# One kernel for a four-layer Perceiver: causal attention by tiles of 128 rows, expert routing by pairs of tiles through a table of token numbers, and cross-attention queries made one tile at a time

## The chip, the cores and the metric

The kernel runs on one core of one Trainium2 chip (trn2). The metric is the device time of one execution in microseconds (us), with the median over runs taken. The profile comes from one further execution of the same program; times inside it are counted from the start of its span.

Engines are named as the profile names them: PE is TensorE (PEld its weight loads), DVE is VectorE, ACT is ScalarE, POOL is GpSimd, SP is SyncE. Each of them runs its instructions in the order of the program that was built for it. SP, ACT and POOL can also issue DMAs.

## The reference, cut to what matters

Sixteen sequences of 64 tokens with 256 features pass through four layers, each with a cross-attention to a context of 1024 tokens of 192 features, a second sublayer and a feed-forward sublayer. All of it is fp32. The parts that the change touches are these:

```python
x = x + L0_xattn(ln(x), ctx)   # one head of 256, 1024 keys
x = x + L0_attn(ln(x))         # causal, 16 heads of 16, q and k RMS-normed over 256 and scaled by ln_w
x = x + L0_ffn(ln(x))          # 8 experts, best 2 of each token, plus a shared expert
x = x + L1_xattn(ln(x), ctx)   # 16 narrow heads of 16, 1024 keys
...
x = x + L1_ffn(ln(x))          # 8 experts, best 1 of each token
...
x = x + L2_ffn(ln(x))          # 8 experts, best 2, at most 160 tokens each
```

Both mixtures of L0 and L1 drop no token: every token goes to each of its experts, and the results come back weighed by the gates.

## The kernel before

The 1024 tokens are eight tiles of 128 rows (`NT = 8`), two sequences in each. The residual `xs` stays in SBUF. One Python object, `Net`, writes the layers one after another. A planner of the framework orders the instructions of every engine by the dependencies and its own estimates of cost. Only inside `manual_schedule(engines={PE})` is PE's order the order in which the code is written; the other engines are still ordered by the planner there.

**L0_first** holds the cross-attention and the causal attention of layer 0. The cross-attention goes by tiles: in step `n` of a loop over `NT + 2` it makes the `scores` of tile `n`, transposes the weights of tile `n - 1` (`keys_first`) and averages the context with them (`averaged`), and projects tile `n - 2` (`by_features`, `output`). Each step reads 3 MB of context, two of the four pairs of context buffers. Between these pieces stand calls of `attn.go()`, seven in a full step. Each of them runs the generator `chunk` in `causal_attention` up to its next `yield`. One chunk of 256 rows (two tiles) is in work at a time, and it starts when both its tiles have their cross-attention. It goes on to the first norm of the feed-forward (`htok`, `hT`) and to the gate logits. PSUM holds one buffer of scores, tag `sc`, which both attentions use in turn, two buffers `o`, two `t` and two `misc`. What is left of the chunks after the loop runs alone until half of them are done, and the first half of the shared expert (`swiglu`, 512 rows) then fills in.

**L0_ffn** routes all 1024 tokens at once. Softmax, the two largest experts, the rank of each token in its expert (`ranks`, a prefix sum by matmul) and the table of blocks (`blocks`: each expert gets a whole number of blocks of 128 slots, 23 blocks in all) are one chain of small DVE operations. `scatter` then writes every token's row of 1 KB to its slot in the DRAM buffer `hs`, which was filled with zeros before. That is one indirect DMA by POOL for each tile and each of the two choices, 16 in all. Each of the 23 blocks gathers its expert's weights by POOL (`wa` 11 KB and `wb` 6 KB a partition, three buffers of each), reads its 128 rows of `hs` by a plain DMA of SP (`hb`, `read_slots`), transposes them to `dT`, and does its matmuls `gu` and `po`. The block's result is written to `ys`, and at the end `take_back` gathers each token's rows from there, 16 indirect DMAs, each followed by one DVE operation that adds to `xs`.

**L1_xattn** starts with the keys and values of the first sequence (`keys_values(0)`), normalizes all eight tiles (`norm_x`), adds the bias to them, and makes the queries of all 1024 rows in two halves (`queries(half)`), with copies `qs[1]` whose partitions are swapped by a DMA. Then it loops over 64 steps of a sequence and four heads. **L1_ffn** routes as L0_ffn does with one choice: 8 scatters, then 15 blocks. **L2_ffn** scatters into fixed slots of `hs`.

Of the kernel before, what the change touches and what calls it, by code (L numbers as in the profile page):

```python
# [10 lines left out]
F32 = mybir.dt.float32  # L11
# [29 lines left out]
class Net:  # L41
# [4 lines left out]
    def __init__(self, tc, a):  # L46
        self.tc, self.nc, self.a = tc, tc.nc, a
        self.flip = 0
        self.n_pT = 2
        self.spare_dve = False  # L50
        self.halves = None

# [173 lines left out]
    def keys_first(self, p):  # L226

        pT = self.lp.tile([128, NK, 128], F32, tag="pT", bufs=self.n_pT, name="pT")
        for g in range(2):
# [4 lines left out]
            if g or self.spare_dve:  # L234
                self.nc.scalar.copy(pT[:, 4 * g : 4 * g + 4, :], ps)  # L235
            else:
                self.nc.vector.tensor_copy(pT[:, 0:4, :], ps)  # L237
        return pT
# [27 lines left out]
    def pack_L0_room(self):  # L266

        self.slot()
        return (
            self.carve(128, 2, 4, 2 * S), self.carve(128, 2, CHUNK), self.carve(128, 2, D),  # L270
            [self.carve(128, 2, D) for _ in range(2)],
            [self.carve(128, 2, 4, S) for _ in range(4)],
            [self.carve(128, 4, 128) for _ in range(4)],
        )

    def L0_first(self):

# [5 lines left out]
        self.spare_dve = True  # L283
        self.more_ctx(self.lp)
# [6 lines left out]
        with self.tc.manual_schedule(engines={mybir.EngineType.PE}):  # L291
# [23 lines left out]
            def scores(i):  # L315
                ctx = ctxs.pop(i) if i in ctxs else fetch(i)
                sc = self.lps.tile([128, KEYS], F32, tag="sc", bufs=1, name="sc")

                for kh in range(2):
                    keys = bass.ts(kh, 512)  # L320
                    for ch in range(2):
                        for par in range(2):
# [4 lines left out]
                            )  # L327
                return ctx, self.exp_rows(sc)

            def averaged(i, ctx, pT):  # L330
                o = self.misc([128, CD + 1])
                for t in range(NK):
                    for par in range(2):
# [3 lines left out]
                        )  # L337
                return self.averages(o, CD + 1)
# [16 lines left out]
            for n in range(NT + 2):  # L355
# [5 lines left out]
                if held is not None:  # L361
                    i, ctx, p = held
                    pT = self.keys_first(p)
# [3 lines left out]
                attn.go()  # L367
# [6 lines left out]
                attn.go()  # L374
                held = got
                if n == NT - 1:

                    nc.sync.dma_start(
                        self.hs.rearrange("(n p) d -> p n d", p=128),
                        self.zero.unsqueeze(1).to_broadcast([128, SLOTS // 128, D]),  # L380
                    )
            del self.ctxT[2:], self.ctx[2:]
            shared = self.swiglu(
                *self.shared, 384, self.add_to_x, 0, lambda: self.lps.tile([128, 512], F32, tag="t", bufs=2, name="gu")
            )
            while attn.go() and attn.done < NT // 2:
                pass
# [4 lines left out]
        self.spare_dve = False  # L392
# [209 lines left out]
    def causal_attention(self, wqkv, wproj):  # L602
# [4 lines left out]
        s = SimpleNamespace(ready=0, next=0, done=0, work=None)  # L607
        sb = self.sb
        room = []

        lw = sb.tile([128, 2, 2], F32, name="lw")
        for c in range(2):
            nc.vector.tensor_scalar(lw[:, c, :], self.pair4, self.col("L0a_lnw", c), None, ALU.mult)
        sel, own = self.pair_masks(sb)
        self.logits = self.act.tile([128, NT, E], F32, tag="logits", name="logits")
        after = {}

        def chunk(g):
            if not room:
                room.extend(self.pack(ahead=False))  # L620
            qs, kT, v, qks, p16, p16T = room
            qs = qs.rearrange("p c b (h q) -> p c b h q", h=2)
            os = []
            for t in range(2):
                x = self.xs[:, 2 * g + t, :]
                mv, rs = self.norm_tile(x, 1e-5)
                os.append(sb.tile([128, D], F32, tag="os", bufs=2, name="os"))
                nc.vector.tensor_scalar(os[t], x, mv[:, 0:1], rs, ALU.subtract, ALU.mult)
            yield
            hT = sb.tile([128, 2, CHUNK], F32, tag="hTs", name="hTs")  # L630
            for t in range(2):
                self.evict(hT[:, :, t * 128 : (t + 1) * 128], self.transposed(os[t]))
            yield
            for t in range(2):
                cols = slice(t * 128, (t + 1) * 128)
                ps = self.misc([128, 2, D])
                self.mm(ps.rearrange("p a b -> p (a b)"), [(hT[:, c, cols], wqkv[:, c, :512]) for c in range(2)])
# [1554 lines left out]
```

## Time and profile before

| what | value |
|---|---|
| median of 3 runs (range) | 3132.53 us (3132.1 to 3138.62) |
| profiled execution, its own time | 3130.54 us |
| its span, first to last instruction | 3128.8 us |
| mean granted TensorE clock | 0.936 |
| PE, DVE, ACT, POOL busy | 2750.3, 1463.2, 1010.6, 310.5 us |
| cross-attention of L0 on PE, first scores | from 29.87 us |
| last `xs` of the causal attention | 259.67 us |
| first matmul of the 23 blocks (`gu<-dT,wa`) | 327.56 us |
| last result of those blocks (`yb`) | 539.18 us |
| both halves of the first scores of L1_xattn there | 599.5 us |
| first matmul of the 15 blocks of L1_ffn (`ph<-dT,wa`) | 1280.98 us |

The time and the span differ by 1.7 us, which lie around the span. The stages follow each other, so each has limits of its own: the page's busy shares are averages over stages of very different kinds. A PE that is busy in a stage is not always at full speed: the granted clock stands beside it.

### The profile page before, as it was taken

The numbers are of one execution on the slowest core, as the hardware profiler recorded it, in microseconds if no ns is written. First come the engines' busy times: TensorE is split into PE (matmuls) and PEld (weight loads), VectorE is DVE, ScalarE is ACT, GpSimd is POOL, SyncE is SP. The second block draws the span as 40 slices with busy tenths as digits, with TensorE's granted clock in tenths as the row PEclk, the third lists the DMA queues.
The fourth block names the chain that finished last, engine by engine and source line by source line (L and its number), as shares of the span: only waits on it lengthen the run. The fifth ranks groups of instructions, "written<-read, shape, count | busy, mean of one in ns | idle before, by whom it ended". The sixth has DMA issues, their size and how long they took to land.

```text
span 3128.8 us, 42567 instructions
## 1 busy us (share of the span) xinstructions
PE 2750.3 (88%) x16976; PEld 1987.6 (64%) x16976; DVE 1463.2 (47%) x2986; ACT 1010.6 (32%) x2160; POOL 310.5 (10%) x425
## 2 busy tenths in 40 slices
PE   6887899699999879788999999496999888887899
PEld 3654787366666536675777776494777566665668
DVE  2553111566666672124444443322345656658591
ACT  1221121255555411122322332021225445455330
POOL 1112221200000010320011000202000000000000
PEclk9897899799999988799999999698999999998999
DMA  9612774201010100761211111373113212122110
GB/s 231 187 41 73 276 275 179 60 31 32 21 32 23 47 1 27 271 217 35 60 42 41 52 51 51 126 248 112 51 41 87 70 41 88 47 72 58 52 37 7
DMA packets 149408, 273.18 MB, mean 87 GB/s; under 512 B 16511, under 2 KB 103258, under 8 KB 142426
## 3 DMA queue, kind: packets, MB, share of 16 engines
q1 hardware_dynamic: 127418, 170.90, 18.6%
q0 software_dynamic: 14784, 93.26, 8.3%
q10 hardware_dynamic: 7008, 6.29, 0.6%
q8 instruction: 134, 2.20, 0.3%
q14 instruction: 64, 0.52, 0.1%
HBM read 247.83 MB, written 20.45 MB: 86 GB/s over the span
## 4 chain that ended last, share of the span: by engine, by line
PE 65%; DVE 10%; issue 7%; ACT 4%; DMA 3%; POOL 2%; SPq 1%; ACTq 0%; DVEq 0%; POOLq 0%
PE misc L65 10%; PE sc L498 8%; PE halves L65 7%; PE gu L65 6%; PE po L65 4%; PE misc L233 4%; PE ps_h L65 4%; PE ps_t L233 3%; PE sc L65 2%; PE misc L844 2%; PE o L892 2%; PE misc L858 2%; DVE x L1832 2%; ACT p L223 2%; PE misc L177 2%
## 5 line engine op out<-in xcount | busy, mean ns | idle before, releaser
L221 DVE TENSOR_REDUCE nmx<-sc 128x1 f32<-128x1024 f32 x264 | 311.7, 1219 | 243.9 <-PE sc L498 148.1
L223 ACT ACTIVATE p<-sc,nmx 128x1024 f32<-128x1024 f32 x264 | 294.0, 1115 | 323.7 <-DVE nmx L221 322.4
L498 PE MATMUL sc<-ctxT,qp 128*128 128x512 f32 (+1 forms) x1024 | 353.9, 600 | 0.0
L498 PEld LDWEIGHTS sc<-ctxT,qp 128*128 128x128 f32 (+1 forms) x1024 | 138.2, 189 | 153.4 <-issue 151.9
L158 POOL TENSOR_TENSOR ln_rs<-ln_ve,nhalf 128x1 f32<-128x1 f32 x120 | 66.7, 561 | 1531.3 <-DVE ln_ve L156 1267.0
L65 PE MATMUL halves<-ctx,pT 128*128 128x193 f32 x1024 | 189.3, 339 | 9.2 <-DVE xs L85 4.1
L65 PEld LDWEIGHTS halves<-ctx,pT 128*128 128x128 f32 x1024 | 177.2, 200 | 12.0 <-DVE xs L85 4.6
L65 PE MATMUL misc<-ctx,pT 128*128 128x193 f32 x1024 | 179.3, 327 | 0.9 <-DVE qT L463 0.9
L65 PEld LDWEIGHTS misc<-ctx,pT 128*128 128x128 f32 x1024 | 167.7, 191 | 2.8 <-DVE qT L463 1.6
L233 PE MATMUL ps_t<-ident,p 128*128 128x128 f32 x1088 | 148.0, 279 | 18.1 <-ACT p L223 10.5
L1832 DVE TENSOR_TENSOR_SCAN x<-da,x 128x512 f32<-128x512 f32 x128 | 152.2, 1213 | 2.1 <-ACT da L1822 1.4
L235 ACT COPY pT<-ps_t 128x512 f32<-128x512 f32 x182 | 103.8, 582 | 149.0 <-PE ps_t L233 148.6
L1822 ACT ACTIVATE da<-rep,al 128x252 f32<-128x252 f32 x256 | 114.8, 498 | 111.1 <-DVE x L1832 90.2
L233 PEld LDWEIGHTS ps_t<-ident,p 128*128 128x128 f32 x1088 | 128.2, 144 | 32.1 <-ACT p L223 13.4
L233 PE MATMUL misc<-ident,p 128*128 128x128 f32 x1024 | 136.8, 279 | 7.1 <-ACT p L223 6.7
L65 PE MATMUL gu<-dT,wa 128*128 128x128 f32 (+1 forms) x1104 | 133.5, 280 | 4.0 <-issue 3.5
L65 PEld LDWEIGHTS gu<-dT,wa 128*128 128x128 f32 (+1 forms) x1104 | 125.7, 185 | 12.7 <-ACT yb L1207 6.3
L233 PEld LDWEIGHTS misc<-ident,p 128*128 128x128 f32 x1024 | 110.1, 141 | 32.7 <-ACT p L223 13.6
L65 PE MATMUL po<-wb,hid 128*128 128x256 f32 x516 | 124.5, 388 | 0.0
L65 PE MATMUL ps_h<-r,w 128*128 128x256 f32 x512 | 115.3, 385 | 0.0
L65 PEld LDWEIGHTS ps_h<-r,w 128*128 128x128 f32 x512 | 97.8, 192 | 16.6 <-issue 2.9
L237 DVE COPY pT<-misc 128x512 f32<-128x512 f32 x128 | 88.2, 689 | 42.5 <-PE misc L233 36.7
(446 smaller groups left out, 4374.7 us busy)
## 6 DMA issues: line engine op xcount, KB each, us to landing
ctx<-in_ctx SPq DMA_DIRECT2D x48, 768.0 KB
ctxT<-in_ctxT SPq DMA_DIRECT2D x48, 512.0 KB
w<-in_L2f_W SPq DMA_DIRECT2D x24, 1024.0 KB
rep<-dus SPq DMA_DIRECT2D x256, 64.0 KB
ctxT<-in_ctxT SPq DMA_DIRECT2D x16, 768.0 KB
ctxT<-in_ctxT SPq DMA_DIRECT2D x96, 128.0 KB
hb<-hs SPq DMA_DIRECT2D x46, 128.0 KB
ys<-yb ACTq DMA_DIRECT2D x46, 128.0 KB
```

The lines of the kernel that those rows point to most:

```text
L65: self.nc.tensor.matmul(out, lhsT, rhs, start=n == 0, stop=n == len(pairs) - 1)
L158: nc.gpsimd.tensor_tensor(rs, ve, self.nhalf, ALU.pow)
L177: self.nc.tensor.transpose(ps[:, c, :], o[:, c * 128 : (c + 1) * 128], self.ident)
L221: self.nc.vector.tensor_reduce(nmx, sc, AX.X, ALU.max, negate=True)
L223: self.nc.scalar.activation(p, sc, AF.Exp, bias=nmx, accum_out=sums)
L233: self.nc.tensor.transpose(ps[:, u, :], p[:, at : at + 128], self.ident)
L235: self.nc.scalar.copy(pT[:, 4 * g : 4 * g + 4, :], ps)
L237: self.nc.vector.tensor_copy(pT[:, 0:4, :], ps)
L498: nc.tensor.matmul(sc[u][:, bass.ts(kh, 512)], qp[n][par][rows, h : h + 2, :].rearrange("p h q -> p (h q)"), ctx[0][rows, at], start=n == ...
L844: nc.tensor.matmul(ps[kh], wk[:, kh, cols], cT[:, bass.ts(kh, 512)], start=True, stop=False)
L1822: nc.scalar.activation(da[:, g, :, 1:], now[j][:, 0, :].rearrange("p (b s) -> p b s", s=S)[:, :, 1:], AF.Exp, scale=al[:, col : col + 1],)
L1832: nc.vector.tensor_tensor_scan(flat, da.rearrange("p g b s -> p (g b s)"), flat, 0.0, ALU.mult, ALU.add)
```

## The change

The causal attention goes by tiles of 128 rows, and up to two tiles are in work at once. The generator `tile` has about twenty pieces, some of them empty, and nine calls of `go()` stand in a full step of the cross-attention, some of them in the middle of its scores and averages. `sc` gets two buffers, the separate `o` goes (its results use `sc` too), and some DVE operations are merged or moved to ACT. The squared norm weight now stands in the queries, and the keys are a plain copy.

After each second tile a generator `routing` is queued behind the tiles. It writes the two tiles' normalized rows to `hs` in the order of the tokens by plain DMAs, makes their logits, softmax, best two and ranks (with a running count `seen`), and scatters the *token numbers*, 4 bytes each, to a DRAM table in which every expert has a region of 1024 places (`place` + `region`).

`blocks` reads one row of 128 token numbers per block from that table by an indirect DMA of POOL that waits for all scatters (`who`), transposes it and keeps it as `tokens`. Each block then gathers its rows of `hs` by POOL with these numbers, in place of SP's plain read. L1_ffn is built the same way, with all its tiles at once. The fixed slots of L2_ffn move to a buffer of their own, `caps`, and only these are filled with zeros.

The shared expert runs in four parts of 256 rows: two in the drain of L0_first, two in L0_ffn. L1_xattn makes the queries of tiles 0 and 1 ahead of its loop and those of tile `i + 2` in the loop, while tile `i` is at work; its bias comes ahead of the first keys.

The core of the diff:

```diff
     def keys_first(self, p, between=lambda: None):
...
+            if not g:
+                between()
...
-                sc = self.lps.tile([128, KEYS], F32, tag="sc", bufs=1, name="sc")
+                sc = self.lps.tile([128, KEYS], F32, tag="sc", bufs=2, name="sc")
...
+                    if not kh:
+                        attn.go()
...
-                    nc.sync.dma_start(
-                        self.hs.rearrange("(n p) d -> p n d", p=128),
-                        self.zero.unsqueeze(1).to_broadcast([128, SLOTS // 128, D]),
-                    )
+                    for n in range(E * CAP // 128):
+                        self.zeros(self.caps[n * 128 : n * 128 + 128])
...
-            while attn.go() and attn.done < NT // 2:
-                pass
+            shared = chain(*(self.shared_part(k) for k in range(2)))
             while attn.go():
                 next(shared, None)
...
+        def tile(i):
...
+            nc.vector.tensor_tensor(qk, ps, rr.unsqueeze(2).to_broadcast([128, 2, D]), ALU.mult)
...
+            nc.scalar.copy(kT, pt[:, 1])
+            yield
+            yield
+            sc = [self.lps.tile([128, 2, 512], F32, tag="sc", bufs=2, name="sc") for _ in range(2)]
...
+            for _ in range(3):
+                yield
...
+            o = self.lps.tile([128, 2, 512], F32, tag="sc", bufs=2, name="o")
...
+            self.add_to_x(i, po)
+            if i % 2:
+                s.behind.append(routing(i // 2))
+            yield
...
+        def routing(g):
...
+            for t in range(2):
+                i = 2 * g + t
+                nc.sync.dma_start(self.hs[i * 128 : (i + 1) * 128], normalized(i, self.htok[:, i, :]))
...
+            for _ in self.route(self.routed, ps, 2 * g):
+                yield
+                yield
 
         def go():
-            if s.work is None and s.next < NC and s.ready >= 2 * s.next + 2:
-                s.work = chunk(s.next)
+            if len(s.work) < 2 and s.next < s.ready:
+                s.work.append(tile(s.next))
                 s.next += 1
-            if s.work is not None and next(s.work, s) is s:
-                s.work = None
-            return s.work is not None or s.next < NC
+            for w in list(s.work):
+                if next(w, s) is s:
+                    s.work.remove(w)
+            if s.behind and next(s.behind[0], s) is s:
+                s.behind.pop(0)
+            return s.work or s.next < NT or s.behind
...
-        def queries(half):
+        def queries(i):
+            mv, rs = self.norm_tile(self.xs[:, i, :], 1e-5)
...
+            nc.gpsimd.tensor_tensor(self.xs[:, i, :], self.xs[:, i, :], bias, ALU.add)
+            yield
...
+            for m in range(2):
+                self.mm(ps[:, m, :], [(wq[:, c, m * 128 : (m + 1) * 128], hT[:, c, :]) for c in range(2)])
...
             for r in range(2):
+                nc.sync.dma_start(qs[i][1][64 * r : 64 * r + 64], qs[i][0][64 - 64 * r : 128 - 64 * r])
...
+            biases()
             for piece in keys_values(0):
                 piece()
-            biases()
-            self.norm_x()
-            for i in range(NT):
-                nc.gpsimd.tensor_tensor(self.xs[:, i, :], self.xs[:, i, :], bias, ALU.add)
-            for half in range(2):
-                queries(half)
+            for i in range(2):
+                for _ in queries(i):
+                    pass
...
+    def route(self, r, logits, first, weighed=None):
...
+        p = self.gate_softmax(logits)
...
+        place = r.place[:, tiles, :]
+        rank = self.ranks(both, r.seen, place)
+        yield
+        rank()
+        for k, m in enumerate(masks):
+            t = self.gate("s_t", n)
+            nc.vector.tensor_tensor(t, place, self.region.unsqueeze(1).to_broadcast([128, n, E]), ALU.add)
+            nc.vector.tensor_tensor(t, t, m, ALU.mult)
+            slot, _ = self.over_experts(t, ALU.add, "s_r")
+            nc.vector.tensor_copy(r.at[k][:, tiles], slot)
+        yield
+        for k in range(len(masks)):
+            self.scatter(r.table, r.at[k], tiles, r.group, lambda i: self.token[:, i : i + 1])
...
-    def blocks(self, count, n_blocks):
+    def blocks(self, seen, table, n_blocks):
+        ps = self.misc([128, E])
+        self.mm(ps, [(self.ones, seen)])
...
+        who = self.lp.tile([n_blocks, 128], F32, name="who")
+        self.behind_scatters(
+            self.gather_rows(who, table.rearrange("(n p) o -> n (p o)", p=128), row[:n_blocks])
+        )
+        ps = self.misc([128, n_blocks])
+        nc.tensor.transpose(ps, who, self.ident[:n_blocks, :n_blocks])
+        tokens = self.lp.tile([128, n_blocks], I32, name="tokens")
+        nc.vector.tensor_copy(tokens, ps)
...
     def block_tokens(self, j):
         hb = self.lp.tile([128, D], F32, tag="hb", bufs=3, name="hb")
-        self.read_slots(hb, slice(j * 128, (j + 1) * 128))
+        self.gather_rows(hb, self.hs, self.tokens[:, j : j + 1])
...
     def L1_ffn(self):
...
+        for i in range(NT):
+            nc.sync.dma_start(self.hs[i * 128 : (i + 1) * 128], self.htok[:, i, :])
...
-        self.scatter(at, "L1f")
```

## The prediction

> **What bounds the kernel now.** I read the page's busy shares, split the span by stages with the windows view, then read each engine's timeline where PE has gaps. Windows (us, then busy us and instructions of PE, PEld, DVE, ACT, POOL; granted clock, DMA share, GB/s):
>
> ```profile
> 30.00:66.00 36.00, 26.31 (x134) 11.36 (x135) 6.05 (x11) 6.01 (x9) 0.55 (x1) 0.86 0.93 235
> 66.00:260.00 194.00, 162.72 (x1170) 110.70 (x1164) 96.10 (x249) 47.37 (x110) 29.21 (x37) 0.84 0.40 115
> 260.00:328.00 68.00, 39.08 (x121) 22.93 (x122) 17.59 (x74) 8.63 (x13) 22.66 (x24) 0.77 0.32 115
> 328.00:539.00 211.00, 206.98 (x1421) 178.03 (x1420) 37.09 (x103) 42.29 (x125) 37.45 (x40) 0.99 0.69 251
> 539.00:600.00 61.00, 29.65 (x96) 13.60 (x96) 28.53 (x74) 6.05 (x11) 26.88 (x37) 0.75 0.31 81
> 600.00:1070.00 470.00, 464.57 (x4388) 290.05 (x4386) 303.70 (x399) 259.57 (x468) 3.83 (x7) 1.00 0.09 27
> ```
>
> The blocks of L0 and the loop of L1_xattn are PE's (98% and 99%, full clock). Context loads bound the first 36 us. The rest, 66 to 328 and 539 to 600, belongs to waits: there PE is 84%, 57% and 49% busy, at a clock of 0.84 to 0.75. PE's timeline names them:
>
> ```profile
> 163.30 1.99 PE L65 MATMUL misc<-rT,sel 8*128 8x256 f32 x8
> 237.71 3.68 PE L65 MATMUL sc<-w 32*128 32x64 f32 x32 [1.48 <-DVE sm L680]
> 251.22 3.78 PE L65 MATMUL misc<-rT,sel 8*128 8x256 f32 x8
> 323.84 0.66 PE L177 MATMUL misc<-ident,hb 128*128 128x128 f32 x2 [23.57 <-DMA hb<-hs]
> 572.20 3.78 PE L844 MATMUL misc<-ctxT,w 128*128 128x512 f32 x4 [26.64 <-DVE kT L849]
> 597.48 2.07 PE L65 MATMUL sc<-kT,qs 32*128 32x512 f32 x4 [4.31 <-DMA qs<-qs]
> ```
>
> The same eight matmuls take 1.99 us in mid-loop and 3.78 us in the drain: gaps also cost clock. The long wait for `hb` is POOL's queue:
>
> ```profile
> 295.88 1.20 POOL L1189 DMA_INDIRECT wa<-in_L0f_w,rows  x1 [33.49 <-issue]
> 297.39 1.01 POOL L1173 DMA_INDIRECT hs<-htok,s_at  x1 [0.30 <-DVE xs L85]
> ...
> 316.57 0.97 POOL L1173 DMA_INDIRECT hs<-htok,s_at  x1 [0.31 <-DMA hs<-htok,s_at]
> 317.85 0.99 POOL L1189 DMA_INDIRECT wb<-in_L0f_w2r,rows  x1 [0.30 <-issue]
> ```
>
> Sixteen scatters at 1.28 us hold it for 20 us. A 1 KB and an 11 KB row cost POOL the same 0.95 to 1.2 us, so 4 bytes should too.
>
> **Part 1: L0_first.** I count PE's work from 66.0 us at full clock, from timeline pieces. Cross-attention: five scores at 3.66, six transposes at 1.07, six averages at 2.85, seven outputs with features at 1.6: 53 us. A chunk of 256 rows: qkv 5.7, three transposes 3.9, scores 4.0, averages 2.2, shares 2.6, projection 2.0, routing's transposes and logits 2.2: 22.6, four times 90. Half the shared expert (24 `gu` at 0.43, 24 `po` at 0.23): 16. Together 159. Before, all this ended at 283, so 217 us: 58 are lost. Two tiles in work, staggered by half a tile, and empty pieces put 2 to 3 calls of other PE work behind each hand-over to DVE or ACT. Counting the calls: nine in a full step, 63 from the first ready tile to the end of the loop; a tile takes 20, so tiles 0 to 4 and most of 5 lie in the loop. That leaves 118 us of work to it; at 87% PE (above the 84% of now, since single waits remain) it ends at 66 + 136 = 202. The drain has 39 us of PE work, but tile 7 is alone at the end, where its chain (about 26 us from norm to sum by its rows) is bare: 44 us. The last sum is at 246, not 260. Bounds: 232 (PE at 97%) and 262 (no overlap gained; both attentions still take turns in `sc`).
>
> The small routing operations of three pairs (about 40 at 0.2 us, 8 us of DVE each) move under this: DVE is at 96 of 194 us, so I cost them at nothing; uncovered they cost 24. `hs` goes out on SP, eight plain DMAs; SP's next loads are two steps ahead.
>
> **Part 2: from the last sum to the first block.** Before: 259.67 to 327.56, 68 us. After, a chain: two norms, transposes, logits 5.4 (259.67 to 265.13 now); softmax to both masks, 4.9 on 64 columns now, 4.3 on 16; running counts, rank matmul, `place`, places 3.0: 12.7. Four scatters 5.1, landing 1.5 (last one ended 317.54, SP issued `hb` at 319.0): 19.3. Then `who` 1.0 + 1.9 (the gather `back`, end of issue 543.06 to use 544.91), transpose and copy 1.0, `hb` 2.8, transpose and eviction 1.1: 27 with empty queues. PE has two parts of the shared expert (16 us) under it.
>
> The queues aren't empty: `rows` is ready at about 13, so weights of 2.25 MB a block (6.1 us at 370 GB/s, what 320 to 332 us moved) are issued while POOL waits for the scatters. Here a row and a rule part. Row: `hb` on SP, issued at 319.3 with five weight gathers outstanding, reached PE 4.5 us later. The Trainium skill, "DMA: Bandwidth & Descriptors", section "Queues, rings and completion order": the engines take turns between queue rows, but within a row's ring descriptors go in order. SP's read shared with the weights; POOL's `who` and `hb` would stand behind them. By the row, block 0 starts at 27 + 2 = 29; by the rule at 43, if three blocks' weights are ahead (18.2 us). No run here shows a small gather behind large ones. The planner issued what was ready, earliest in the code first; so I put `wa`, `wb` of block 0 ahead of `who` and those of block 1 ahead of `hb`: 35. First block at 246 + 35 = 281 instead of 327.6: **46 less**, 31 to 62 likely. The two new waits stand in POOL's order: `who` for the scatters, `hb` for `tokens`, up to 1.5 and 4 us. Behind them are the weights of blocks 1 and 2, needed 9 and 18 us later, so this delay is covered by block 0.
>
> **Part 3: the blocks.** POOL gets 23 and 15 gathers at 1.25 us more (37 of 211 us busy now), SP loses as many. The next `hb` buffer is free when an old block is transposed, before its weights' buffer, so it should be issued first. Costed at nothing; its cover is the three-deep `hb`.
>
> **Part 4: L1_xattn.** Before, the loop runs from 597.5, since `kT` waited in DVE's order behind nearly all additions of `take_back`, then 9.6 us of PE for all norms' transposes and queries. After, with two tiles' norms only, POOL's 16 gathers take 20.5 us (542.1 to 562.6), `kT` follows at about 564, the rest of keys and values 9.6, two tiles' queries with their swap DMA 5: 578, 19 earlier. But six tiles' queries (8 matmul records at 0.12 and transposes, 1.5 us) enter a loop where PE is full: 9 back. Net 11. From 8 to 28, if `kT` is ordered early.
>
> **Part 5: L1_ffn.** Places no longer wait for `first` (3 us sooner), still 8 scatters, then `who`, `tokens`, and `hb` behind two blocks' weights: first matmul at 1279 to 1283, now 1280.98. Zero, from 4 gained to 8 lost. L2_ffn's chain stays; zeroing 1.3 instead of 3.4 MB has DMA slack beside it.
>
> **Sum.** 46 + 11 + 0 = 57. The profiled execution is 3130.5 with 1.7 us around its span: 3073.5 there; the median is 2.0 higher: 3075.
>
> **Rivals.**
> *Less overlap* (0.22): drain and waits stay, last sum at 262, tail 35, L1_xattn 8: 31 + 8 less a few for L1_ffn, about 3096. For it: one shared `sc` pair, DVE's fixed order. Against: the waits named above are single hand-overs, which another tile fills.
> *More* (0.18): last sum at 236, no weights ahead, `kT` early: 328 - 265 = 63, 28, 3: about 3040. For it: little PE work is needed in the tail. Against: POOL issued weights early before.
> *Slower* (0.05): in the blocks `hb` stands in POOL's ring behind weights that wait for a buffer, so a block starts only when later weights have landed. Over 38 blocks the gain of 57 is gone at 1.5 us each, that is a pace of 10.7 for 9.2 us in L0; 2 us each give 3151. For it: SP's queue had no such neighbour. Against: three buffers and DMA at 0.69.
> *Nothing in sum* (0.01): POOL's and DVE's order put the last pair's routing behind the shared expert and `take_back`, as now, so that parts 1 and 4 come back as waits: 3132.
>
> **Numbers.** The forecast case has 0.54; its range is 3060 to 3090. With the others, 3040 to 3108 leaves about 2 in 10 out. 0.2% (6 us) is about what a measurement can tell: faster 0.94, same 0.01, slower 0.05.
>
> **What would show it.** Last `xs` of tile 7 near 246 with no `sc` wait over 2 us; POOL with four, not 16, scatters before `wa`; `hb` at about 33 us after that sum; block pace 9.2; the L1_xattn loop from about 532 (597.5 less 46 and 19), and longer by 9. Wrong if PE in 66 to 200 stays at 84%, if `who` lands after all three weights, if blocks wait for `hb`, or if `kT` still ends the start of L1_xattn.

## The result, and the profile after

The change made the kernel a little faster: 3119.81 us in the median of 20 runs, against 3132.30 us for 20 runs of the kernel before. The ratio is 0.9967, with a 95% interval from 0.9957 to 0.9977. The forecast was 3075 us with a range from 3040 to 3108: the sign was right, and 57 us were forecast where about 12 came. The profiled execution has a span of 3123.7 us (3128.8 before) and lies some 6 us above the median of its kernel, as one sample may. One of the 20 runs of the changed kernel lasted 5600.49 us; it counts as slow and stands outside the ratio.

The same views as before, now of the changed kernel. First the stages (us, then busy us and instructions of PE, PEld, DVE, ACT, POOL; granted clock, DMA share, GB/s), cut where the stages end now:

```profile
66.00:264.00 198.00, 164.80 (x1296) 110.60 (x1291) 104.33 (x326) 59.45 (x139) 41.50 (x50) 0.85 0.43 101
264.00:303.00 39.00, 21.83 (x91) 17.49 (x89) 14.11 (x76) 4.43 (x10) 13.29 (x14) 0.78 0.59 136
303.00:514.00 211.00, 206.70 (x1424) 177.10 (x1424) 37.36 (x104) 42.84 (x126) 57.70 (x62) 1.00 0.71 260
514.00:566.00 52.00, 21.83 (x80) 11.20 (x82) 21.91 (x66) 4.47 (x7) 23.95 (x33) 0.69 0.22 64
566.00:1052.00 486.00, 478.94 (x4492) 300.65 (x4490) 317.13 (x433) 262.45 (x474) 6.74 (x11) 0.99 0.10 29
```

The blocks (third row) are as long as before with 20 us more of POOL. L1_xattn's loop (last row, cut wide) is 10 us longer: from the end of its first scores to its last `o<-pT,v` it takes 487.1 us, before 477.0. The tail of L0_first (second row) went from 68 to 39 us. But the first row, which was to end at 246, is still at a clock of 0.85 and PE 83% busy, and the start of L1_xattn (fourth row) has PE at 42%. PE's timeline names what it waited for:

```profile
208.74 2.11 PE L698 MATMUL pt<-ident,w 128*128 128x128 f32 x8 [7.70 <-ACT w L691]
257.37 2.12 PE L698 MATMUL pt<-ident,w 128*128 128x128 f32 x8 [4.21 <-ACT w L691]
295.16 0.29 PE L1246 MATMUL misc<-ident,who 23*128 23x23 f32 x1 [11.60 <-DMA who<-table,row_p]
295.38 7.09 PE L67 MATMUL misc<-w,hid 128*128 128x256 f32 x24
302.31 0.38 PE L179 MATMUL misc<-ident,hb 128*128 128x128 f32 x2
303.37 5.72 PE L67 MATMUL gu<-dT,wa 128*128 128x128 f32 x48 [0.68 <-issue]
541.35 2.07 PE L67 MATMUL misc<-w,bv 128*128 128x256 f32 x4 [27.87 <-DVE bv L815]
565.62 2.08 PE L67 MATMUL sc<-kT,qs 32*128 32x512 f32 x4 [0.26 <-DMA qs<-qs]
1253.86 0.25 PE L1246 MATMUL misc<-ident,who 15*128 15x15 f32 x1 [27.77 <-DMA who<-table,row_p]
```

Two of these waits are for `who`, the new gather from the table. POOL's timeline shows that it was not late by its own issue: between `wa` and `who` POOL stands still for 9.28 us (10.46 us in L1_ffn, the last line, where the profile names the scatters as what it waited for).

```profile
278.89 0.95 POOL L1269 DMA_INDIRECT table<-token,route_at  x1 [0.30 <-issue]
280.15 1.00 POOL L1291 DMA_INDIRECT wa<-in_L0f_w,rows  x1 [0.30 <-issue]
290.43 1.20 POOL L1291 DMA_INDIRECT who<-table,row_p  x1 [9.28 <-issue]
291.92 0.97 POOL L1291 DMA_INDIRECT wb<-in_L0f_w2r,rows  x1 [0.30 <-issue]
295.94 0.94 POOL L1291 DMA_INDIRECT hb<-hs,tokens  x1 [3.04 <-DVE tokens L1248]
1249.10 0.91 POOL L1291 DMA_INDIRECT who<-table,row_p  x1 [10.46 <-DMA table<-token,route_at]
```

The last scatter's issue ends at 279.84, and `who` starts at 290.43: 10.6 us for the landing (until the written bytes are in memory and a reader may start), where the prediction had 1.5. In L1_ffn it is 11.7 us.

Every kernel below is compared by these stages, each taken from one profile of its own, in us: the last `xs` of L0_first; from there to the first matmul of L0's blocks (the tail); from the last `yb` of the blocks (its start on ACT) to the first `sc<-kT,qs` of L1_xattn; and in L1_ffn from the first operation on the gate logits to the first `ph<-dT,wa`.

| kernel | last sum | to first block | last `yb` to first scores | L1_ffn, logits to first block |
|---|---|---|---|---|
| before | 259.67 | 67.9 | 52.9 | 37.0 |
| changed | 264.30 | 39.1 | 50.6 | 49.9 |
| changed, second profile (`after_again`) | 262.11 | 38.2 | 50.9 | 48.4 |
| `orders` | 258.47 | 41.3 | 46.4 | 40.0 |
| `rows512` | 254.16 | 31.2 | 51.1 | 39.5 |
| `pitch512` | 253.15 | 31.1 | 50.9 | 39.5 |
| `spread` | 254.55 | 39.3 | 51.6 | 34.8 |
| `l1x_early` | 254.57 | 38.6 | 44.7 | 49.7 |
| `l1x_early2` | 253.67 | 38.1 | 37.9 | 47.9 |
| `drain_bare` | 245.03 | 52.9 | 50.3 | 48.5 |
| `route_late` | 237.61 | 63.2 | 50.7 | 48.9 |
| `chain_late` | 247.76 | 54.9 | 50.8 | 48.8 |
| `best` | 251.47 | 30.9 | 38.1 | 33.7 |
| `best_one` | 245.83 | 42.2 | 38.0 | 34.0 |

### The profile page after: what moved, and what is told of

It is laid out like the page before. It is cut to its first block, busy times and chain, and to the rows that moved or that the text cites. A ratio compares the mean times of both kernels' runs of the same rounds, so it can differ in the third digit from the quotient of the medians.

```text
span 3123.7 us, 43069 instructions
## 1 busy us (share of the span) xinstructions
PE 2741.2 (88%) x17116; PEld 1987.1 (64%) x17116; DVE 1473.8 (47%) x3103; ACT 1019.0 (33%) x2187; POOL 349.9 (11%) x468
## 4 chain that ended last, share of the span: by engine, by line
PE 71%; DVE 11%; DMA 5%; ACT 5%; issue 3%; POOL 2%; SPq 2%; another core or an unknown queue 0%; ACTq 0%; DVEq 0%; POOLq 0%
PE misc L67 12%; PE sc L501 8%; PE halves L67 7%; PE gu L67 7%; PE po L67 5%; PE misc L235 4%; PE ps_h L67 4%; PE ps_t L235 3%; PE sc L67 2%; PE misc L862 2%; PE o L913 2%; PE misc L876 2%; PE ph L67 2%; ACT p L225 2%; DVE x L1942 2%
## 5 line engine op out<-in xcount | busy, mean ns | idle before, releaser
L235 PEld LDWEIGHTS misc<-ident,p 128*128 128x128 f32 x1024 | 111.2, 141 | 32.5 <-ACT p L225 12.9
L237 ACT COPY pT<-misc 128x512 f32<-128x512 f32 x128 | 75.0, 586 | 107.7 <-PE misc L235 107.2
```

The source lines that it names most:

```text
L235: self.nc.tensor.transpose(ps[:, u, :], p[:, at : at + 128], self.ident)
```

## The experiments

All kernels start from the changed one.

### Order of work on PE: `orders`

```diff
 # L0_ffn and L1_ffn: the shared parts and the gates' products go to blocks() as `meanwhile`
         self.behind_scatters(self.gather_rows(who, ...))
+        meanwhile()
         ps = self.misc([128, n_blocks])
         nc.tensor.transpose(ps, who, ...)
 # L1_xattn
-            biases()
             for piece in keys_values(0):
                 piece()
+            biases()
```

> Three orders of work on PE are changed, each in a stage of its own: in L0_ffn the last two parts of the shared expert are written ahead of the transpose of who; in L1_xattn the product of biases() comes behind keys_values(0); in L1_ffn the eight transposes of gates with their products with b2 are written ahead of the transpose of who. Theory 'order' (PE stood behind an instruction that waited, with work behind it that was ready): last causal sum to first block 39.1 -> about 32 us (the 7.1 us of misc<-w,hid no longer follow who); last yb to first scores of L1_xattn 52.1 -> 38 to 42 us (keys and values, 15 us of PE, lie under take_back); logits to first block of L1_ffn 49.9 -> about 40 us. In sum 26 to 30 us less than the changed kernel: about 3092, ratio to before 0.987. Rival 'next wait': DVE's own order puts kT behind the sixteen additions as it did before, and the weights or hb end the other two waits: L1_xattn's start stays over 48, each of the two starts of blocks loses less than 3 us, in sum under 10 us.

Measured: 3109.42 us, ratio to before 0.9939 (0.9917 to 0.9961). The three edits had three different fates.

In L1_ffn the theory held, 49.9 to 40.0: eight transposes of gates and their products had stood behind the transpose of `who` in PE's order, ready all the time. In L0_ffn nothing was gained (41.3 for 39.1): with the shared expert out of the way PE waits for `hb`. And at the start of L1_xattn 4 us came instead of 10 to 14. In the changed kernel PE itself stood there: the product of the bias, `misc<-w,bv`, headed its order and waited 27.87 us for `bv`, which DVE makes behind the last addition of `take_back`. With the bias behind the keys PE makes the first 3.7 us of keys and values early, and then another wait holds it. From `orders`, PE, then ACT:

```profile
298.59 1.09 PE L179 MATMUL misc<-ident,hb 128*128 128x128 f32 x4 [8.78 <-DMA hb<-hs,tokens]
```

```profile
538.44 0.69 ACT L868 ACTIVATE kT<-misc,vecs 128x512 f32<-128x512 f32 x1 [27.04 <-DVE xs L1176]
```

`hb` was issued at 290.30, behind `wb`, `wa`, `wb` in POOL's order, and PE had it 8.3 us later. And ACT, which has nothing else to do there, does not write the first `kT` until the last addition of `take_back`. Nothing in the computation asks for that; the next experiments on L1_xattn follow it.

### The landing of the scatters: `rows512`, `pitch512`

Is it the size of the writes, where they lie, or the wait for several queues as such? Both kernels write into a buffer of their own, and `who` still waits for the scatters.

```diff
 # rows512
-            self.scatter(r.table, r.at[k], tiles, r.group, lambda i: self.token[:, i : i + 1])
+            self.scatter(self.wide, r.at[k], tiles, r.group, lambda i: self.htok[:, i, :128])
 # pitch512: 4 bytes, slots 512 bytes apart
-            nc.vector.tensor_copy(r.at[k][:, tiles], slot)
+            nc.vector.tensor_scalar(r.at[k][:, tiles], slot, 128.0, None, ALU.mult)
```

> The scatters write rows of 512 bytes (half a token's features) to a DRAM buffer of their own instead of 4 bytes to the table; the table stays as it was filled, so every slot of a block reads the row of zeros, and the amount of work is the same. Theory 'small writes': the 10.6 us (tail) and 11.7 us (L1_ffn) from the end of the last scatter's issue to the gather who come from writes of 4 bytes; here they are under 3 us, the first weights no longer trickle in, first block of L0 39.1 -> about 31 us after the last sum, first block of L1_ffn 49.9 -> about 41 us after the logits, and DVE's stop of 5.4 us at 199.5 is gone. Rival 'waiting on many queues': the time is what any gather needs that waits for four to eight indirect DMAs; it stays 10 to 12 us whatever the size, and so does DVE's stop.

> The scatters write the same 4 bytes, but to slots 512 bytes apart in a DRAM buffer of their own; the table stays as it was filled, so every slot of a block reads the row of zeros, and the amount of work is the same. Theory 'size': each write of 4 bytes is slow by itself, so last scatter to who stays at 10 to 12 us. Theory 'neighbours': writes to slots side by side in one line of memory wait for each other; with slots apart it falls under 4 us. Rival 'waiting on many queues': 10 to 12 us here and with 512-byte rows alike.

Measured: 3092.9 and 3090.2 us in one run each, with 3130.64 us for the kernel before, measured beside them. POOL in `rows512`, then in `pitch512`:

```profile
268.74 0.96 POOL L1269 DMA_INDIRECT wide<-htok,route_at  x1 [0.30 <-issue]
270.00 1.00 POOL L1291 DMA_INDIRECT wa<-in_L0f_w,rows  x1 [0.30 <-DMA wide<-htok,route_at]
272.12 1.20 POOL L1291 DMA_INDIRECT who<-table,row_p  x1 [1.11 <-issue]
```

```profile
267.73 0.96 POOL L1269 DMA_INDIRECT wide<-token,route_at  x1 [0.31 <-issue]
271.00 1.20 POOL L1291 DMA_INDIRECT who<-table,row_p  x1 [1.01 <-issue]
```

From the end of the last scatter's issue to `who` it is 2.4 us with rows of 512 bytes and 2.3 us with 4 bytes at a distance of 512. So size is not the cause and neither is the wait for several DMAs: 4-byte writes are slow where they are neighbours. The tail is 31 us in both, below the 35 of the prediction. Their total times must be read with care, since all blocks work on zeros here and the clock is a little higher (0.941 and 0.943, the changed kernel 0.934).

### A table without neighbours: `spread`

Slot s of row n lies at 64 s + n, so successive ranks of an expert are 256 bytes apart. This one computes everything.

```diff
-            nc.vector.tensor_copy(r.at[k][:, tiles], slot)
+            # m = -8191 * floor(slot / 128), by rounding
+            nc.vector.scalar_tensor_tensor(r.at[k][:, tiles], slot, 64.0, m, ALU.mult, ALU.add)
...
+        who = self.lp.tile([128, S], F32, name="who")
+        self.behind_scatters(nc.sync.dma_start(who, table.rearrange("(p n) o -> p (n o)", p=128)))
+        nc.vector.tensor_tensor(pick, pick, who.unsqueeze(1).to_broadcast(wide), ALU.mult)
+        nc.vector.tensor_reduce(named, pick, AX.X, ALU.add)
```

> The changed kernel with another layout of the table, and nothing else: the slots of a block lie 256 bytes apart (slot s of row n at 64 s + n), so that successive ranks of an expert are no neighbours; SP reads the whole table of 32 KB as 128 rows of 64, and two DVE operations on 128x1472 (about 1.6 us each) pick each block's column, in place of the gather who and its transpose. Theory 'neighbours' (writes of 4 bytes within 64 to 256 bytes of each other wait for each other): last scatter to the read of the table about 2.5 us, read 2 us, picking 3.5 us, hb: last causal sum to first block of L0 39.1 -> 31 to 33 us, logits to first block of L1_ffn 49.9 -> about 42, the last sum itself 4 us earlier since DVE's stop is gone; in sum 18 to 22 us less than the changed kernel, ratio to before 0.990. Rival 'the same line up to 512 bytes' : the landing stays 10 us, and with the longer picking it is 2 to 4 us slower than the changed kernel, ratio 0.998.

Measured: 3090.75 us, ratio 0.9884 (0.9864 to 0.9904). The gain is at least the one expected (by the two ratios some 26 us on the changed kernel, for 18 to 22), but it lies elsewhere: the tail gained nothing for 6 to 8, the last sum came 10 us earlier for 4, and L1_ffn gained 15 for 8. POOL, SP, DVE and PE of `spread`:

```profile
269.61 2.22 POOL L1272 DMA_INDIRECT table<-token,route_at  x1 [0.31 <-issue]
```

```profile
273.16 0.33 SPq L1246 DMA_DIRECT2D who<-table  x1
```

```profile
280.16 1.69 DVE L1247 TENSOR_TENSOR pick<-pick,who 128x1472 f32<-128x1472 f32 x1 [8.04 <-DMA who<-table]
```

```profile
282.31 2.93 PE L67 MATMUL misc<-w,hid 128*128 128x256 f32 x6 [7.67 <-DVE hid L1130]
293.83 5.72 PE L67 MATMUL gu<-dT,wa 128*128 128x128 f32 x48 [0.68 <-issue]
```

The read of the table is issued 1.3 us after the last scatter: at 256 bytes the landing is short too. But the read itself takes 7.0 us, with two gathers of weights issued around it (in two later kernels with the same read it takes 1.9 and 6.6), and DVE waits for it with the shared expert's `hid` behind it in its order; PE then has that work left when `hb` is there. The tail stays at 39.3. L1_ffn, with its gates' products free under the scatters, goes to 34.8.

### The start of L1_xattn: `l1x_early`, `l1x_early2`

The change claims `take_back`'s buffers at the very start of L0_ffn (`rooms_back()`), and it makes the queries' tiles small. The suspicion is that the first `kT` now lies in memory that those buffers hold until their last reader is done: in `orders` ACT's first `kT` waits for just that addition, though it doesn't use its result. `l1x_early` claims the buffers behind the blocks, puts `biases()` behind the keys and gives all first evictions to ACT; `l1x_early2` also moves the slots that `take_back`'s gathers read.

```diff
 # l1x_early
-        self.rooms_back()          # start of L0_ffn
...
+        self.rooms_back()          # behind the 23 blocks
         for i in range(NT):
             for k in range(2):
                 y = self.take_back(at[k], i)
 # l1x_early2
-        at = self.lp.tile([128, NT], I32, name=f"{name}_at32")
+        at = self.back_at.pop(0)   # in the room of route_at
```

> The changed kernel with the start of L1_xattn freed in three ways: take_back's three buffers are claimed behind the blocks of L0 and not ahead of them, biases() comes behind keys_values(0), and the keys and values of the first sequence are all evicted by ACT. Theory 'room' (in the run before this one ACT's first kT waited 27.0 us for the last addition, because it lies where take_back's buffers were claimed): kT now waits for the blocks' gathers alone, PE makes keys and values under take_back, and only two tiles' queries follow the last addition: last yb to first scores of L1_xattn 52.1 (47.5 in the run with the orders changed) -> 33 to 39 us; ratio to before about 0.992. Rival 'weights' (kT also lies where the blocks' weights and hb were, and ctxT's own transfers come late): it stays above 45.

> As the run before it on the start of L1_xattn, and one thing more: the slots that take_back's gathers read lie outside the memory that the first kT takes. In that run ACT's kT still waited 26.7 us for the last gather `back`. Theory 'room': that was the same reuse of memory by another tile; with it gone PE makes the keys and values of the first sequence under the 26 us of take_back, and after the last addition only biases() and two tiles' queries are left: last yb to first scores 45.8 -> 33 to 37 us. Rival 'order': ACT's kT is no longer held, but something else of the stage (the transfers of ctxT, the queries' norms) keeps PE until after the last addition: above 42 us.

(These expectations count to the second four of the score matmuls, 1.5 us later than the table above.) Measured: `l1x_early` 3101.42 us, ratio 0.9926 (0.9910 to 0.9943); `l1x_early2` 3097.64 us in one run, with 3126.95 for before. ACT's first `kT` in the one and in the other, and PE's product of the bias in the other:

```profile
530.34 0.69 ACT L870 ACTIVATE kT<-misc,vecs 128x512 f32<-128x512 f32 x1 [26.68 <-DMA back<-ys,s_at]
```

```profile
504.91 0.69 ACT L870 ACTIVATE kT<-misc,vecs 128x512 f32<-128x512 f32 x1 [2.60 <-PE misc L864]
529.70 2.05 PE L67 MATMUL misc<-w,bv 128*128 128x256 f32 x4 [15.05 <-issue]
```

In `l1x_early` the addition no longer ends the wait, but the last gather does, by the slots that it reads. With these moved `kT` waits for PE alone, the keys and values lie under `take_back`, and last `yb` to first scores falls to 37.9 us. So memory held `kT`, since moving what else lay there set it free. But both were needed, the memory and the order of code: in `l1x_early2` too the bias comes only at 529.70, 27.8 us after the last `yb`, and with the bias ahead of the keys PE would have stood until then, as it did in the changed kernel. Counted as in the expectations the two kernels come to 46 and about 40 us, where 33 to 39 and 33 to 37 were expected.

### L0_first: `drain_bare`, `route_late`, `chain_late`, `after_again`

Three kernels take something out of L0_first. `route_late` lets the pairs' routing begin only when no tile is in work (the two parts of the shared expert in the drain then read rows that are not yet written; their amount of work is the same). `chain_late` moves of it only the DVE chain, the rank products and the scatters.

```diff
 # drain_bare
             while attn.go():
-                next(shared, None)
+                pass
 # route_late
-            if s.behind and next(s.behind[0], s) is s:
+            if not s.work and s.next == NT and s.behind and next(s.behind[0], s) is s:
 # chain_late
-            for _ in self.route(self.routed, ps, 2 * g):
+            nc.vector.tensor_copy(lg, ps)
+            s.late.append((lg, g))     # route() behind the last tile
```

> The two parts of the shared expert that fill the drain of L0_first (16 us of PE at full clock) are moved behind it, to the other two. Theory 'chain' (two tiles in work: the rest of tile 5 and then all of tile 7 are one chain of hand-overs, and PE has room): the last sum stays within 4 us of 264.3 and the clock of the drain falls further. Rival 'PE' (the drain is 39 us of PE work, stretched to 50 by a clock of 0.7 to 0.8, with the shared expert between the pieces): the last sum comes 12 us or more earlier, near 250. In both, first block later than the last sum by 39 us plus what of the 16 us does not fit under the wait for the table, 0 to 10 us.

> The routing of the pairs is begun only when the last tile's sum is done, so nothing of it lies between the tiles; its whole length, four pairs one after the other, then follows the last sum. Theory 'covered' (the prediction's: routing costs L0_first nothing): the loop and drain keep their length but for the stop of DVE behind the scatters, so the last sum comes 3 to 6 us before that of the changed kernel. Rival 'routing sits in the drain's chain' (about 40 small operations of DVE a pair, and PE's short products between the tiles): the last sum comes 10 us or more earlier. In both the first block is later than in the changed kernel by three more rounds of routing, 30 to 45 us.

> The changed kernel once more, as the control for the stages of L0_first. Theory 'its profile was a slow sample there' (three kernels with the same code in L0_first have their last sum at 253.7 to 258.5 us, the profile of the changed kernel at 264.3; its first loop steps show a clock of 0.95 for 1.00): last sum at 253 to 259. Rival 'the code elsewhere moves it' : 263 to 265 again.

> Of the routing only the chain of small DVE operations, the rank products and the scatters are moved behind the last tile; norms, transposes and gate logits of the pairs stay between the tiles. Theory 'chain' (the 15 us by which the loop of L0_first was shorter without any routing, 177.5 for 192.8, belong to the DVE operations between the tiles): the loop ends near 180, the last sum near 240. Rival 'PE work and its waits' (transposes, logits and the waits for htok stand in PE's order): the loop ends at 188 to 192 and the last sum at 250 or later; DVE's operations were covered as the prediction said. First block later in both.

The last sums: changed (two profiles), `drain_bare`, `route_late`, `chain_late`, each from its own DVE timeline:

```profile
264.30 0.42 DVE L87 TENSOR_TENSOR xs<-xs,misc 128x256 f32<-128x256 f32 x1 [1.31 <-PE misc L67]
```

```profile
262.11 0.42 DVE L87 TENSOR_TENSOR xs<-xs,misc 128x256 f32<-128x256 f32 x1 [3.29 <-PE misc L67]
```

```profile
245.03 0.42 DVE L87 TENSOR_TENSOR xs<-xs,misc 128x256 f32<-128x256 f32 x1 [3.17 <-PE misc L67]
```

```profile
237.61 0.42 DVE L87 TENSOR_TENSOR xs<-xs,misc 128x256 f32<-128x256 f32 x1 [2.16 <-PE misc L67]
```

```profile
247.76 0.42 DVE L87 TENSOR_TENSOR xs<-xs,misc 128x256 f32<-128x256 f32 x1 [2.98 <-PE misc L67]
```

`after_again` missed its expectation, and its rival, that code elsewhere moves this stage, came nearer: the changed kernel ends late in its second profile too, while `orders`, `l1x_early` and `l1x_early2`, with the same code of L0_first, end at 253.7 to 258.5. The three late ones (258.5 to 264.3) are those in which DVE stands still in the loop (last section), the others not; that this is the cause is not shown. So differences below 10 us between kernels say little here.

With this in mind: the routing costs L0_first 16 to 27 us (237.6 against 253.7 to 264.3), nearly all of it in the loop. The loop's last matmul on `onT` ends at 177.5 in `route_late` and at 187.2 in `chain_late`; with the routing in place it ends at 201.0 and 199.7 in the changed kernel, and at 191.6 to 195.2 in `orders`, `l1x_early` and `l1x_early2`. So norms, transposes and logits cost it some 10 us, and the DVE chain with its products and scatters 4 to 14. Neither theory of `chain_late` was right alone.

The shared expert costs the drain 10 to 11 us: from the end of the loop to the last sum it is 63.3 in the changed kernel and in `orders`, 61.8 to 62.4 in the other three, and 52.3 in `drain_bare`. The theory 'chain' fell by its number, but not altogether, since these 52.3 us are left with no shared expert at all. PE from 200 to 240 and from 240 to 265 in the changed kernel, then from 200 to 240 in `drain_bare`:

```profile
200.00:240.00 40.00, 30.61 (x191) 24.04 (x190) 18.58 (x50) 14.81 (x29) 5.85 (x7) 0.80 0.02 7
240.00:265.00 25.00, 19.50 (x166) 14.10 (x165) 14.40 (x51) 5.59 (x14) 7.22 (x8) 0.71 0.11 22
```

```profile
200.00:240.00 40.00, 29.38 (x255) 19.46 (x254) 22.86 (x79) 11.10 (x29) 11.02 (x13) 0.71 0.03 8
```

Over its whole drain `drain_bare` has PE busy for 36.3 of 52.3 us at a granted clock of 0.67; the changed kernel for 48.4 of 63.3 at 0.77.

The three kernels give most of their gain back behind the last sum, where the work that they moved now stands (second column of the table): 3112.5, 3120.0 and 3121.8 us in one run each, with 3130.6, 3125.1 and 3134.7 for the kernel before, measured beside them.

### What they come to together: `best`, `best_one`

`best` has the spread table, the shared expert's rest and the gates' products ahead of the picking, and `l1x_early2`; `best_one` has one part of the shared expert in the drain in place of two.

```diff
 # best, blocks(): ahead of DVE's wait for the table
+        meanwhile()
         nc.vector.tensor_tensor(pick, pick, who.unsqueeze(1).to_broadcast(wide), ALU.mult)
 # best_one
-            shared = chain(*(self.shared_part(k) for k in range(2)))
+            shared = chain(*(self.shared_part(k) for k in range(1)))
```

> All that the runs point to, on top of the changed kernel: the table with slots 256 bytes apart, read by SP; the last two parts of the shared expert ahead of the picking in DVE's and PE's order; the gates' products with b2 under the scatters in L1_ffn; the start of L1_xattn freed as in the run beside this one. Theory (the three waits add up, since they lie in stages of their own): against the kernel with the spread table (3090.8) 3 to 6 us less at L0's blocks, 14 to 18 less at L1_xattn: 3067 to 3075, ratio to before 0.981 to 0.984. Rival 'given back' (L1_xattn's loop or the next stage starts at a lower clock, or waits for the context instead): at most 8 us less than 3090.8, ratio 0.986 or more.

> As the kernel beside it, but only one of the shared expert's four parts lies in the drain of L0_first and three behind it. Theory 'chain in the drain, room in the tail' (without any of the four the last sum came 10 us earlier than in runs of the same chip state, and PE stands idle for 12 us or more while the table is written, read and picked): last sum 5 us earlier, the 8 us more of PE work under the table's time, first block 2 to 5 us earlier than in the kernel beside it. Rival 'PE is full in the tail': first block at the same time or later.

Measured: `best` 3075.84 us, ratio to before 0.9837 (0.9823 to 0.9852); `best_one` 3083.42 us, 0.9860 (0.9844 to 0.9875). The gains of the stages add up in `best`, at the lower edge of what was expected. Its five runs lie between 3071.21 and 3080.94 us, and the profile is of the fastest. SP, DVE and PE of `best`, then DVE of `best_one`:

```profile
268.81 0.33 SPq L1254 DMA_DIRECT2D who<-table  x1
```

```profile
270.72 1.69 DVE L1256 TENSOR_TENSOR pick<-pick,who 128x1472 f32<-128x1472 f32 x1 [1.79 <-DMA who<-table]
```

```profile
281.44 0.41 PE L179 MATMUL misc<-ident,hb 128*128 128x128 f32 x2 [3.09 <-DMA hb<-hs,tokens]
282.41 8.65 PE L67 MATMUL gu<-dT,wa 128*128 128x128 f32 x48 [0.56 <-issue]
```

```profile
270.00 1.69 DVE L1256 TENSOR_TENSOR pick<-pick,who 128x1472 f32<-128x1472 f32 x1 [6.95 <-DMA who<-table]
```

The shared expert is done when `hb` comes, and the tail is 30.9 us. In `best_one` the last sum comes 5.6 us earlier, at 245.8, but the first block at 288.06 instead of 282.41. The rival forecast that, but its reason, a PE that is full in the tail, is not shown: the read of the table takes 6.6 us in this profile and 1.9 in that of `best`, and PE stands still for 4.4 us around it. Without that, by estimate, the two first blocks would lie within 1.5 us of each other. What decides between 1.9 and 7 us was not tried.

## Why the prediction was wrong, step by step

**Part 1, last sum at 246: wrong by 18 (16 in the second profile).** Two steps failed. The first is the drain, sized at 44 us as 39 us of PE work at full clock beside a bare chain of tile 7; it took 63.3. The amount of work was about right: PE was busy for 48.4 us at a granted clock of 0.77, by estimate 37 us at full clock. But the clock made 48 of it, and the waits between the links of the chain made another 15. The chain itself was undersized too: with no shared expert, so 16 us less work, the drain still takes 52.3 us. The pieces of the shared expert do not all lie beside the chain, but partly between its links (10 to 11 us). The prediction had shown the same eight matmuls at 1.99 and 3.78 us, and then counted the drain at full clock.

The second is the routing "at nothing". It named DVE's idle half as the cover and 24 us as the price without it; `route_late` puts the price at 16 to 27. Here a DVE that was busy for half of the time did not cover operations that stand in a chain of hand-overs and that PE waits for in its own order. That the loop met its number (202 forecast, 201.0 measured) was luck: it would have ended at 177.5 without the routing that was costed at nothing, and the same code ended it at 191.6 to 195.2 in other profiles.

**Part 2, 35 us from last sum to first block: 39.1, by wrong terms that partly cancel.** Places took 10.6 us for 12.7; the four scatters 5.0 as forecast; the landing 10.6 for 1.5; `who` 4.7 for 2.9; from there to the first block 8.2 for 4.9, since PE made 7.1 us of the shared expert's products first. The mis-sized term is the landing, taken from the nearest row, a scatter of 1 KB rows: the row was near in instruction, not in where the bytes fall (`pitch512`, 2.3 us). Of the 8 us added for weights ahead of `who` and `hb` at most half was needed: with a landing of 2.3 us the tail is 31, where empty queues were put at 27. POOL's own wait for the landing kept `wb` behind `who`. On the rule in the Trainium skill, "DMA: Bandwidth & Descriptors", section "Queues, rings and completion order": in `orders`, where `wb`, `wa`, `wb` were issued just ahead, `hb` took 8.3 us, not the 4.5 of SP's row. In this one case the rule was the better guide. First block 24 us earlier (303.37 for 327.56) instead of 46: 18 from part 1 and 4 from here.

**Part 3, nothing: right.** First block to last `yb` 210.2 us, before 211.6.

**Part 4, 19 earlier and 9 longer: half right.** The loop is 10 us longer. The start gained 6 (58.3 to 52.1 from last `yb` to the full scores). The step that failed is "the rest of keys and values 9.6". It took over from the kernel before that the first half of the keys and values, 6.4 us of PE, lies under `take_back`:

```profile
539.08 1.98 PE L844 MATMUL misc<-ctxT,w 128*128 128x512 f32 x4
544.42 1.14 PE L865 MATMUL misc<-w,ctxT 64*128 64x256 f32 x8
```

But the change puts the bias ahead of the first keys, and its product waits until 27.8 us after the last `yb`. In the changed kernel bias, keys and values all follow that, 17.7 us for 9.6, and then the queries, 6.6 for 5. Moving the bias alone did not help much, because memory then held `kT` until about the same moment (`orders`). No line of the profile of before could show that. With both freed, in `l1x_early2`, the second four score matmuls end 41.7 us after the last `yb`, in the kernel before 60.4: 18.7 earlier. That this is the 19 of the forecast is chance, since the forecast had `kT` behind the gathers, and for an early `kT` it said 28.

**Part 5, nothing, at most 8 lost: 12.9 lost** (37.0 to 49.9). The landing again, 11.7 us, and a wait taken over by PE: the transpose of `who` came to head PE's order, with 15 us of gates' products behind it that had run under the scatters before. Either one mended gives back about 10 us (`orders`, `rows512`), both give 15 to 16 (`spread`, `best`).

The profiles' sum: 24 gained at L0's first block, 32 at L1_xattn's scores, 22 behind its loop, 10 at L1_ffn's blocks, 5 at the end. The last 5 are lost at the start of L2_xattn, where the same instructions ran at a lower granted clock (16 score matmuls took 6.64 us for 5.52, at 0.88 for 1.00); that is seen, and its cause was not tried. `best` gains 51 us on the kernel before it was measured beside (3126.95), close to the 57 of the forecast, but not by the forecast's steps: its drain still takes 61.8 us, and it gains 3 us in L1_ffn, which the forecast had left as it was. Of the rivals, *less overlap* (3096) was the nearest, with its drain and waits that stay.

## What to carry to other kernels

Before a small operation is costed at nothing, ask who waits for it and in which order that engine's instructions stand: a half idle engine need not cover a link of a chain. A drain in which one tile is left should be sized by its chain and at the clock that such stretches show, not by the work in it. A new wait must be followed to what stands behind it in the same order, here gates' products, keys and a shared expert that were ready all along. And when the shape of a tile changes, look at whose memory the next stage's first tiles now take over: a buffer claimed earlier or made smaller can hold up a stage that the change never mentions.

## What the runs showed of the hardware that was not expected

- Indirect writes of 4 bytes land 9.3 to 12.0 us after the last one's issue, in both FFNs of the eight profiles here in which neighbouring ranks are neighbours in memory. At a distance of 512 bytes it is 2.3 us and at 256 it is 1.3 to 1.8, where rows of 512 bytes take 2.4. Distances between 4 and 256 bytes were not tried, and why neighbours are slow is open. While they are under way the weights issued behind them move slowly: 34 to 57 GB/s from 280 to 290, 322 GB/s from 292 to 296 in the changed kernel.
- The same read of the 32 KB table on SP's queue took 1.9 us in `best`, 6.6 in `best_one` and 7.0 in `spread`, each time with gathers of weights issued on POOL within about 1.5 us of it.
- In two profiles of the changed kernel, in `orders` and in `drain_bare`, DVE stood still behind the second pair's scatters although its instruction uses PE's result alone, and went on 10 to 12 us after their issue ended; in `l1x_early` and `l1x_early2`, with the same scatters, it did not. From the changed kernel and `l1x_early`:

```profile
204.95 1.29 DVE L683 TENSOR_TENSOR sm<-sc,causal 128x512 f32<-128x512 f32 x2 [5.41 <-remote]
```

```profile
192.93 1.28 DVE L683 TENSOR_TENSOR sm<-sc,causal 128x512 f32<-128x512 f32 x2
```

  The cause stays open.
- An indirect DMA's issue on POOL, else 0.9 to 1.2 us, took 1.68 to 2.22 us in `spread` and `best` where it fell together with a DVE operation of 1.68 us on 128x1472 elements (the row at 269.61 above is one).
